# The last rounds of a gather kept free of other stages, and weights loaded within them

## The chip, the cores and the metric

The kernel runs on one core of one Trainium2 chip. The metric is the device time of one execution in microseconds. The core has five engines that run side by side and wait for each other through semaphores: PE (matmuls), DVE and ACT (elementwise work), POOL (which issues the indirect DMAs here) and SP (which issues all other DMAs). Each works through its own stream of instructions in order.

## What is computed

The input x has shape (4, 256, 64, 64): four images of 256 channels and 4096 pixels, in float32. Four layers are applied, each as x = x + layer(groupnorm(x)):

```python
x = x + _L0_conv_ref(_gn(x), ...)   # 1x1 conv, deformable 3x3 sampling, projection, gated feed-forward
x = x + _L1_conv_ref(_gn(x), ...)   # linear attention with a depthwise 5x5 convolution
x = x + _L2_conv_ref(_gn(x), ...)   # 3x3 convolution with binarised weights
x = x + _L3_conv_ref(_gn(x), ...)   # attention over a 2x2 max-pooled image
```

What matters of layer 0 is its second half. A bilinear sampling reads 9 points in each of 4 groups for every pixel, at offsets that the network has computed; the result is projected to 256 channels and added. Then come the gate and the feed-forward:

```python
x2 = _bn(inp + dout, bn2_g, bn2_b, bn2_m, bn2_v, 3)
s = x2.mean((1, 2))
s = jax.nn.relu(s @ se_down_w.T + se_down_b)
s = jax.nn.sigmoid(s @ se_up_w.T + se_up_b)
x3 = x2 * s[:, None, None, :]
hmid = jax.nn.leaky_relu(jnp.einsum('nhwc,oc->nhwo', x3, fc1_w) + fc1_b, SLOPE)
m = jnp.einsum('nhwc,oc->nhwo', hmid, fc2_w) + fc2_b
```

The mean runs over all pixels of an image, so the feed-forward of an image can begin only when its sampling has ended.

## The kernel before

The program is written as Python generators, one for each stage of each image, and a function that takes turns between them. `sample(n)` is the sampling of image n in 288 rounds: 16 blocks of 18 rounds. In a round, POOL issues four indirect DMAs (L607, tile `g`, a ring of seven buffers, so that POOL can be at most seven rounds ahead of PE), and PE turns the four gathered tiles into weighted sums with eight matmuls (L614, into the PSUM banks `acc` and `dp` in turn, two rounds to a bank). After two rounds ACT copies the bank (L619, `at`), PE transposes it (L624), ACT spreads it into `dT` (L634), and at the end of a block PE projects it (L647, `po`), DVE adds it to the image (L653, L654) and ACT finishes it (L658), which also leaves its sum for the mean (`ssum`), and SP writes it out (L661, `x2`). The weights `wm` of the rounds are made by ACT (L599), some rounds ahead; for the first rounds of a sampling all 32 activations stand at its start.

`beside(steps, number, *works)` walks over the rounds of a sampling, and after each round lets the other stages emit their instructions. Each work is a tuple of a generator, its total cost, and the share of the rounds at which it begins and ends. A work emits as long as it has spent less of its cost than its share says; once the share has reached its end, all that is left of it is emitted at once. Inside `ordered()` the order of emission is the order of the instructions on PE, DVE, ACT and POOL. SP's order is left to the scheduler.

The samplings run one after another. Sampling 0 has the first convolutions of the other images beside it. Beside sampling 1 run `binarise`, the feed-forward and the linear attention of image 0. Beside samplings 2 and 3 run the feed-forward and the linear attention of the image before (`behind`), and the 3x3 convolution and the pooled attention of the image before that (`second`). The feed-forward has the rounds up to the share 0.22 (`BEGUN`, round 63), `linear` and `second` the rest up to the end. After sampling 3, a last `beside` over 900 steps without a sampling takes the feed-forward and the linear attention of the last image and what is left of the others.

The emission of `feedforward` begins with two pools of buffers on the right side of SBUF, which take the place of those that `linear` has left, and with four loads: `f1` and `f2` (8 KB in each of 128 partitions, 1 MB each; both stand as `f` in the profile), `sd` and `su`. Then DVE reduces the mean (L712), PE takes it through `sd` (L716) and `su` (L723), ACT makes the gate (L718, L724) and scales `f1` by it (L727), and the blocks follow: L752 and L762 on PE. In the linear attention the last steps on PE are `den` (L938), `rden` (L951) and the projection (L960); in the pooled attention they are L1315, L1327, L1333 and L1343. The weights of the 3x3 convolution, `w2`, are loaded by one DMA of 3 MB (L1051).

Of the kernel before, what the change touches and what calls it, by code (L numbers as in the profile page):

```python
# [18 lines left out]
N, C, H, W = 4, 256, 64, 64  # L19
# [20 lines left out]
CONVOLVE, OFFSETS, BINARY = NB * 9 + 26, 60, 92  # L40
FEED = NB * 40 + 8
LINEAR, LAST = 956, 582
STEPS, BEGUN = 900, 0.22
CONV2, POOLED = 191, 376.5
CONV, SECOND = 150, 568
EPS_BN = 1e-5
# [26 lines left out]
class Net:  # L73
# [625 lines left out]
    def feedforward(self, n, ssum, st):  # L699
        nc, tc, a = self.nc, self.tc, self.a  # L700
        with tc.tile_pool(name=f"fa{n}", bufs=1, side="right") as sp, \
                tc.tile_pool(name=f"fb{n}", bufs=2, side="right") as bp:
            f1 = sp.tile([P, KT, 4 * C], F32, name="f1")
            nc.sync.dma_start(f1, a["fc1_wT"])
            f2 = sp.tile([P, 4 * KT, C], F32, name="f2")
            nc.sync.dma_start(f2, a["fc2_wT"])
            sd = sp.tile([P, KT, 64], F32, name="sd")
            nc.sync.dma_start(sd, a["se_down_wT"])
            su = sp.tile([64, C], F32, name="su")
            nc.sync.dma_start(su, a["se_up_wT"])  # L710
            mean = sp.tile([P, KT], F32, name="mean")
            nc.vector.tensor_reduce(mean, ssum, AX.X, ALU.add)  # L712
            nc.vector.tensor_scalar(mean, mean, 1.0 / HW, None, ALU.mult)
            ps = self.ps()
            for k in range(KT):
                nc.tensor.matmul(ps[0:64, 0:1], sd[:, k], mean[:, k:k + 1], start=k == 0, stop=k == KT - 1)  # L716
            dn = sp.tile([64, 1], F32, name="dn")
            nc.scalar.activation(dn, ps[0:64, 0:1], AF.Relu, bias=self.vec("se_down_b")[0:64])  # L718
            yield 2
            ex = sp.tile([P, KT], F32, name="ex")  # L720
            for m in range(KT):
                ps = self.ps()
                nc.tensor.matmul(ps[:, 0:1], su[:, m * P:(m + 1) * P], dn, start=True, stop=True)  # L723
                nc.scalar.activation(ex[:, m:m + 1], ps[:, 0:1], AF.Sigmoid, bias=self.vec("se_up_b", m))  # L724

            for k in range(KT):
                nc.scalar.activation(f1[:, k], f1[:, k], AF.Identity, scale=ex[:, k:k + 1])  # L727
            yield 6

            waits = []  # L730

            def leave():
                if waits:
                    waits.pop()()

            def hidden(hm, m, ps, t):
                nc.vector.scalar_tensor_tensor(hm[:, m], ps, self.vec("fc1_b", m), t, ALU.add, ALU.max)  # L737

            def total(b, m, ps, xy):
                nc.vector.tensor_tensor(xy[:, m], xy[:, m], ps, ALU.add)  # L740
                if m == KT - 1:
                    self.stats(st, xy, b)
                    nc.sync.dma_start(self.x3_d[n][:, :, b * 512:(b + 1) * 512], xy)

            for b in range(NB):
                x2 = self.block(bp, self.x2_d[n], b, "x2f")
                xy = self.block(bp, self.xy_d[n], b, "xyf")
                hm = bp.tile([P, 4 * KT, 512], F32, name="hm", bufs=1)
                for m in range(4 * KT):
                    ps = self.ps()  # L750
                    for k in range(KT):
                        nc.tensor.matmul(ps, f1[:, k, m * P:(m + 1) * P], x2[:, k], start=k == 0, stop=k == KT - 1)  # L752
                    t = bp.tile([P, 512], F32, name="lk")
                    nc.scalar.activation(t, ps, AF.Identity, bias=self.low1[:, m:m + 1], scale=SLOPE)  # L754
                    leave()
                    waits.append(partial(hidden, hm, m, ps, t))
                    yield 2.5
                leave()
                for m in range(KT):
                    ps = self.ps()  # L760
                    for k in range(4 * KT):
                        nc.tensor.matmul(ps, f2[:, k, m * P:(m + 1) * P], hm[:, k], start=k == 0, stop=k == 4 * KT - 1)  # L762
                        if k % 4 == 3:
                            leave()
                            yield 5
                    waits.append(partial(total, b, m, ps, xy))
            leave()
# [580 lines left out]
    def run(self):  # L1348
        self.setup()
        tile = lambda name, shape: self.cp.tile(shape, F32, name=name)  # L1350
        ssum = [tile(f"ssum{n}", [P, KT, NBLK]) for n in range(N)]
        st = {i: [tile(f"st{i}{n}", [P, KT, NB, 6]) for n in range(2)] for i in (1, 2, 3)}

        feed = lambda n: self.feedforward(n, ssum[n], st[1][n % 2])
        linear = lambda n: self.layer1(n, st[1][n % 2], st[2][n % 2])

        conv = lambda n, side="left": self.layer2(n, st[2][n % 2], st[3][n % 2], side)
        pooled = lambda n, wide=False: self.layer3(n, st[3][n % 2], wide)

        def second(n):  # L1360
            yield from conv(n)
            yield from pooled(n)

        def beside(steps, number, *works):


            spent, open_ = [0] * len(works), set(range(len(works)))

            def advance(share):
                for j in sorted(open_):  # L1370
                    work, total, lo, hi = works[j]
                    while j in open_ and lo <= share and spent[j] < total * (share - lo) / (hi - lo) or share >= hi:
                        cost = next(work, None)
                        if cost is None:
                            open_.discard(j)
                        if not cost:
                            break
                        spent[j] += cost

            for i, _ in enumerate(steps, 1):  # L1380
                advance(i / number)
            while any(works[j][3] <= 1 for j in open_):
                advance(1)

        rounds = NBLK * BR
        E = mybir.EngineType
        ordered = lambda: self.tc.manual_schedule(engines={E.PE, E.DVE, E.Activation, E.Pool})
        behind = lambda n: [(feed(n), FEED, 0, BEGUN), (linear(n), LINEAR, BEGUN, 1)]
        with self.tc.tile_pool(name="gather", bufs=2, side="left") as self.gp, \
                self.tc.tile_pool(name="samp", bufs=2, side="left") as self.sp:  # L1390
            with self.tc.tile_pool(name="pw", bufs=1, side="right") as wp, \
                    self.tc.tile_pool(name="pa", bufs=1, side="right") as sp, \
                    self.tc.tile_pool(name="pb", bufs=2, side="right") as bp:
                w = self.weights(wp)

                pads, used = [], []  # L1400
                convolved = (y for i in range(1, N) for y in self.convolve(i, w, sp, bp, pads, used))
                shifted = lambda first, last: (self.shifts(first, last, w["mw"], bp, pads, used), (last - first) * OFFSETS)
                beside(range(64), 64, (self.convolve(0, w, sp, bp, pads, used), CONVOLVE, 0, 1), (*shifted(0, 1), 0.3, 1))
                with ordered():
                    beside(self.sample(0, ssum[0]), rounds, (convolved, (N - 1) * CONVOLVE, 0, 0.96), (*shifted(1, N * NCH), 0, 1))
            with ordered():
                beside(self.sample(1, ssum[1]), rounds, (self.binarise(), BINARY, 0, 0.2), *behind(0))
                for n in range(2, N):
                    beside(self.sample(n, ssum[n]), rounds, *behind(n - 1), (second(n - 2), SECOND, BEGUN, 1))
        self.idle, self.alone, self.spare = cycle(["acc", "dp"]), True, True  # L1410
        rest = pooled(N - 2)
        with ordered():
            beside(range(STEPS), STEPS, (feed(N - 1), FEED, 0, 0.27), (linear(N - 1), LAST, 0.27, 1), (conv(N - 2), CONV2, 0.27, 0.53), (rest, POOLED, 0.53, 1.02))
        self.spare = False
        self.idle = cycle(["acc", "dp", "vk"])
        fours = self.layer2_fours(N - 1, st[2][1], st[3][1])
        beside(range(STEPS), STEPS, (fours, CONV, 0, 1), (rest, 60, 0, 1))

        self.banks = cycle(["mm", "mm", "mm", "vk"])
        for _ in pooled(N - 1, True):  # L1420
            pass
# [94 lines left out]
```

## Time and profile before

| what | us |
|---|---|
| median of 3 runs | 7441.21 (7437.45 to 7445.19) |
| the profiled execution | 7427.54 |
| its span | 7425.7 |
| PE busy | 5885.9 (79%) |
| DVE busy | 4870.1 (66%) |
| ACT busy | 3564.6 (48%) |
| POOL busy | 4928.8 (66%) |

The span is what the instructions cover; the execution has 1.8 us around it. The four samplings can be told from POOL's gathers: the first begins at 138.5 us, the others at 1598.0, 3051.6 and 4504.2, and the last gather ends at 5976.5. The mean of a feed-forward (L712) is taken at 1617.1, 3073.8, 4548.7 and 6019.9. These four places are called seams in what follows. A row of the timeline gives the start, the length, the engine, the line, the operation with output and inputs, how many such instructions were merged, and in brackets how long the engine sat idle before it and what ended this. A row of the waits gives who waited for what, the sum in us, the number of waits and the longest. A row of busy times by stretch gives the stretch, its length, the busy time of PE, PEld, DVE, ACT and POOL, the share of PE's clock that was granted, the share of the DMA engines' time and GB/s.

### The profile page before, as it was taken

How to read it: one execution, taken by the hardware profiler on the slowest of the kernel's cores; microseconds unless marked ns; L12 is line 12 of the kernel's file. 1: busy time of each engine (PE TensorE's matmuls, PEld its weight loads, DVE VectorE, ACT ScalarE, POOL GpSimd, SP SyncE). 2: the span in 40 equal slices, each digit the busy share in tenths (PEclk: the TensorE clock that was granted, in tenths of full speed). 3: DMA queues.
4: the chain of work that ended last, by engine and by line, in shares of the span. 5: the costliest groups of instructions: out<-in, count | busy, mean ns of one | idle time of the engine just before them, and what ended most of it. 6: DMA issues, size and time to landing. Idle time of an engine off the chain costs nothing. (4 is left out here: it accounts for less than half of the span.)

```text
span 7425.7 us, 98944 instructions
## 1 busy us (share of the span) xinstructions
PE 5885.9 (79%) x35584; PEld 3436.3 (46%) x35584; DVE 4870.1 (66%) x6099; ACT 3564.6 (48%) x10807; POOL 4928.8 (66%) x4850
## 2 busy tenths in 40 slices
PE   5676766569777777898877788988777889977889
PEld 2333333334433333345655444456554444844477
DVE  6455552644488777326989883269998833999863
ACT  2444444445554444455556554554565532655425
POOL 1777777777777777777777776777777710865410
PEclk7776776779877767898988889989889899988899
DMA  6564654666544445555554445555544431210141
GB/s 187 148 191 144 176 173 137 174 183 190 178 127 125 125 125 147 168 156 167 159 155 139 141 147 187 153 167 159 156 142 145 146 115 65 81 54 34 49 124 49
DMA packets 743149, 1037.48 MB, mean 140 GB/s; under 512 B 352000, under 2 KB 457856, under 8 KB 741248
## 3 DMA queue, kind: packets, MB, share of 16 engines
q0 software_dynamic: 221184, 604.27, 27.8%
q1 hardware_dynamic: 521472, 426.87, 19.0%
q8 instruction: 280, 4.59, 0.3%
q14 instruction: 213, 1.74, 0.1%
HBM read 857.44 MB, written 173.33 MB: 139 GB/s over the span
## 5 line engine op out<-in xcount | busy, mean ns | idle before, releaser
L607 POOL DMA_INDIRECT g<-tab,sl x4608 | 4403.3, 956 | 1571.9 <-issue 1285.6
L179 DVE SCALAR_TENSOR_TENSOR agg<-pad,vec,agg 128x1024 f32<-128x1024 f32 x2280 | 2934.3, 1287 | 64.3
L599 ACT ACTIVATE wm<-sl,con 128x48 f32<-128x48 f32 x6144 | 1496.1, 363 | 24.9 <-DMA sl<-sd 11.8
L614 PE MATMUL dp<-g,wm 128*32 128x128 f32 x9216 | 664.2, 317 | 312.2 <-DMA g<-tab,sl 308.7
L614 PE MATMUL acc<-g,wm 128*32 128x128 f32 x9216 | 664.2, 318 | 298.5 <-DMA g<-tab,sl 285.5
L614 PEld LDWEIGHTS dp<-g,wm 128*32 128x32 f32 x9216 | 324.4, 119 | 664.4 <-DMA g<-tab,sl 493.4
L614 PEld LDWEIGHTS acc<-g,wm 128*32 128x32 f32 x9216 | 325.3, 120 | 661.4 <-DMA g<-tab,sl 452.5
L1102 PE MATMUL ps<-xd,w 128*128 128x256 f32 x2304 | 547.1, 386 | 47.9 <-ACT kt L891 38.6
L1102 PEld LDWEIGHTS ps<-xd,w 128*128 128x128 f32 x2304 | 430.5, 193 | 131.7 <-ACT kt L891 40.3
L752 PE MATMUL ps<-x2f,f 128*128 128x512 f32 x1024 | 479.0, 613 | 4.7 <-ACT f L727 4.0
L762 PE MATMUL ps<-hm,f 128*128 128x512 f32 x1024 | 467.7, 604 | 0.0
L837 PE MATMUL ps<-xr,qw 128*128 128x512 f32 x768 | 442.8, 706 | 31.2 <-DMA xr<-x 20.9
L737 DVE SCALAR_TENSOR_TENSOR hm<-ps,vec,lk 128x512 f32<-128x512 f32 x256 | 191.5, 751 | 372.8 <-ACT lk L754 369.2
L619 ACT COPY at<-dp 128x256 f32<-128x256 f32 x288 | 107.3, 373 | 679.9 <-PE dp L614 668.6
L619 ACT COPY at<-acc 128x256 f32<-128x256 f32 x288 | 107.2, 372 | 594.0 <-PE acc L614 584.0
L754 ACT ACTIVATE lk<-ps,low 128x512 f32<-128x512 f32 x256 | 175.7, 688 | 363.1 <-PE ps L752 359.2
L1333 PE MATMUL ps<-gt,pT 128*128 128x129 f32 x2048 | 303.3, 307 | 34.4 <-ACT pT L1329 32.2
L1333 PEld LDWEIGHTS ps<-gt,pT 128*128 128x128 f32 x2048 | 286.7, 219 | 87.5 <-ACT pT L1329 48.7
L647 PE MATMUL po<-dT,ow 128*128 128x288 f32 x1024 | 299.3, 440 | 25.5 <-ACT dT L642 11.6
L1315 PE MATMUL s<-ph,th 128*128 128x512 f32 x512 | 280.7, 659 | 44.9 <-DVE ot L955 13.8
L201 POOL TENSOR_TENSOR ak<-ak,m 128x1024 f32<-128x1024 f32 x96 | 229.0, 2385 | 119.3 <-ACT m L197 115.7
L201 POOL TENSOR_TENSOR av<-av,m 128x1024 f32<-128x1024 f32 x96 | 227.8, 2373 | 113.2 <-ACT m L197 109.2
(286 smaller groups left out, 8337.6 us busy)
## 6 DMA issues: line engine op xcount, KB each, us to landing
g<-tab,sl POOLq DMA_INDIRECT x4608
x<-x SPq DMA_DIRECT2D x112, 512.0 KB
xr<-x SPq DMA_DIRECT2D x96, 512.0 KB
tab<-xo SPq DMA_DIRECT2D x192, 128.0 KB
x<-in_x SPq DMA_DIRECT2D x32, 512.0 KB
y<-yc SPq DMA_DIRECT2D x32, 512.0 KB
yb<-y SPq DMA_DIRECT2D x64, 256.0 KB
x<-yb SPq DMA_DIRECT2D x64, 256.0 KB
```

The lines of the kernel that those rows point to most:

```text
L179: nc.vector.scalar_tensor_tensor(to, s, wt, acc, ALU.mult, ALU.add)
L201: nc.gpsimd.tensor_tensor(acc, acc, made[t - 1], ALU.add)
L599: nc.scalar.activation(wm[:, :, :, o], blocks[b][:, r:r + WR, G:], AF.Copy, scale=self.con("own")[:, o:o + 1])
L607: nc.gpsimd.indirect_dma_start(out=g[:, i, :], out_offset=None, in_=table, in_offset=bass.IndirectOffsetOnAxis(ap=sl.bitcast(I32)[:, r, i: ...
L614: nc.tensor.matmul(acc[32 * i:32 * i + 32, :], wm[:, r4, 4 * i + 2 * x:4 * i + 2 * x + 2, :], g[:, i, x * P:(x + 1) * P], start=x == 0, st ...
L647: nc.tensor.matmul(po[m][:, 0:BR * OB], self.ow[:, k, m * P:(m + 1) * P], dT[b][:, k].rearrange("p r o -> p (r o)"), start=k == 0, stop=k ...
L752: nc.tensor.matmul(ps, f1[:, k, m * P:(m + 1) * P], x2[:, k], start=k == 0, stop=k == KT - 1)
L762: nc.tensor.matmul(ps, f2[:, k, m * P:(m + 1) * P], hm[:, k], start=k == 0, stop=k == 4 * KT - 1)
L837: nc.tensor.matmul(ps, qw[:, k, m * P:(m + 1) * P], x[:, k], start=k == 0, stop=k == KT - 1)
L1102: nc.tensor.matmul(ps[:, e], w[:, k, t, 2 * half + e, m * P:(m + 1) * P], v[:, 2 * half + e, k, t:t + 8], start=i % 6 == 0, stop=i % 6 == 5)
L1315: nc.tensor.matmul(s[i], tv[:, 4 * b + j], ph[:, i * 512:(i + 1) * 512], start=True, stop=True)
L1333: nc.tensor.matmul(ps[:, 0:P + 1], pT[:, m], gt[:, m], start=m == 0, stop=m == 7)
```

## The change

A third mark, `END` = 0.98, takes the place of 1 as the end of `linear` and of `second` beside the samplings. 0.98 of 288 rounds is 282.2, so what is left of them is emitted after the 283rd round. The feed-forwards are made once, in a list, instead of by a function, and `feedforward` has one more stop, after its four loads. `behind` has a third work: the feed-forward of the next image, with the cost 1, from `END` on; its end of 2 is never reached, so only its first step is emitted, the pools and the four loads. The next `beside` takes up the same generator after them.

```diff
-STEPS, BEGUN = 900, 0.22
+STEPS, BEGUN, END = 900, 0.22, 0.98
...
             su = sp.tile([64, C], F32, name="su")
             nc.sync.dma_start(su, a["se_up_wT"])
+            yield 1
             mean = sp.tile([P, KT], F32, name="mean")
...
-        feed = lambda n: self.feedforward(n, ssum[n], st[1][n % 2])
+        feeds = [self.feedforward(n, ssum[n], st[1][n % 2]) for n in range(N)]
...
-        behind = lambda n: [(feed(n), FEED, 0, BEGUN), (linear(n), LINEAR, BEGUN, 1)]
+        behind = lambda n: [(feeds[n], FEED, 0, BEGUN), (linear(n), LINEAR, BEGUN, END), (feeds[n + 1], 1, END, 2)]
...
-                    beside(self.sample(n, ssum[n]), rounds, *behind(n - 1), (second(n - 2), SECOND, BEGUN, 1))
+                    beside(self.sample(n, ssum[n]), rounds, *behind(n - 1), (second(n - 2), SECOND, BEGUN, END))
...
-            beside(range(STEPS), STEPS, (feed(N - 1), FEED, 0, 0.27), (linear(N - 1), LAST, 0.27, 1), (conv(N - 2), CONV2, 0.27, 0.53), (rest, POOLED, 0.53, 1.02))
+            beside(range(STEPS), STEPS, (feeds[N - 1], FEED, 0, 0.27), (linear(N - 1), LAST, 0.27, 1), (conv(N - 2), CONV2, 0.27, 0.53), (rest, POOLED, 0.53, 1.02))
```

The new line in `feedforward` moves all lines behind it by one: L716 of before is L717 of the changed kernel, L1343 is L1344.

## The prediction

> **What bounds the kernel now.** I read the groups by line first, then the waits of PE and of POOL sampling by sampling, then the timelines of PE and POOL at the seams between samplings. The page's costliest groups:
>
> ```profile
> L607 POOL DMA_INDIRECT g<-tab,sl x4608 | 4403.3, 956 | 1571.9 <-issue 1285.6
> L179 DVE SCALAR_TENSOR_TENSOR agg<-pad,vec,agg 128x1024 f32<-128x1024 f32 x2280 | 2934.3, 1287 | 64.3
> ```
>
> POOL issues one gather every 0.95 + 0.30 = 1.25 us, so a round (four gathers) costs it 5.0 us and a sampling (288 rounds) 1441 us; four samplings fill 138 to 5976 us almost without a hole. It looks as if POOL were the bound. PE's waits, by sampling, say otherwise. Sampling 1 from round 63 on (window 1920 to 3050):
>
> ```profile
> PE dp L614 <- DMA g<-tab,sl: 109.5, 156, 1.9
> PE acc L614 <- DMA g<-tab,sl: 98.3, 130, 3.6
> ```
>
> There PE starves for gathered data 286 times: POOL leads. In the same stretch of samplings 2 and 3 (3380 to 4540, 4870 to 6012) no such wait stands among the longest; what stands there is the other stages' work, here of sampling 3:
>
> ```profile
> PE pt L1327 <- ACT pe L1321: 29.0, 15, 4.2
> PE dp L624 <- ACT at L619: 25.3, 11, 9.7
> PE acc L624 <- ACT at L619: 23.7, 12, 8.7
> PE ps L1102 <- ACT kt L891: 19.7, 3, 18.2
> ```
>
> and the busy time of the two stretches (time, PE, PEld, DVE, ACT, POOL):
>
> ```profile
> 3374.00:4542.00 1168.00, 944.04 (x6834) 613.00 (x6832) 985.68 (x1166) 632.80 (x2022) 879.15 (x922) 0.89 0.52 152
> 4856.00:6013.00 1157.00, 934.20 (x6809) 611.23 (x6809) 983.09 (x1160) 630.64 (x2014) 847.44 (x888) 0.89 0.51 151
> ```
>
> PE 81% and DVE 84%, coupled by waits on each other: from round 64 of sampling 2 on the two run behind POOL, and POOL is held by its ring of seven `g` buffers. At the end of sampling 3 POOL is done well before PE:
>
> ```profile
> 5975.51 0.95 POOL L607 DMA_INDIRECT g<-tab,sl  x1 [0.30 <-issue]
> ...
> 6005.57 0.65 PE L614 MATMUL dp<-g,wm 128*32 128x128 f32 x16
> 6006.15 3.70 PE L960 MATMUL ps<-ot,pw 128*128 128x512 f32 x8
> 6010.98 1.98 PE L1343 MATMUL ps<-m,ww 128*128 128x512 f32 x4 [1.13 <-ACT m L1338]
> 6012.80 0.38 PE L624 MATMUL dp<-ident,at 128*128 128x128 f32 x2
> 6014.46 4.15 PE L647 MATMUL po<-dT,ow 128*128 128x288 f32 x16 [1.28 <-ACT dT L642]
> 6027.79 0.56 PE L716 MATMUL ps<-mean,sd 128*64 128x1 f32 x4 [9.18 <-DMA su<-in_se_up_wT]
> ```
>
> PE takes the last round 30 us after its gather (6006.2 against 5976.5), ends the other stages (L1343) at 6013.0, then projects the last block, and waits 9.2 us for the feed-forward's weights. At the seam 2 to 3 the same order costs POOL its only long stops:
>
> ```profile
> 4553.78 0.94 POOL L607 DMA_INDIRECT g<-tab,sl  x1 [13.57 <-PE acc L614]
> ...
> 4564.49 0.94 POOL L607 DMA_INDIRECT g<-tab,sl  x1 [6.01 <-DMA xyf<-x]
> ```
>
> **What the Trainium skill says.** "Perfetto Trace Analysis", Optimization Strategy: where the most contended engine changes over time, take the gaps within the regime concerned. The trace agrees: POOL's 20 us of stops lie at a seam, inside a stretch that PE and DVE set. "TensorE: Matmul & The Clock Gate", The mechanism: matmuls start and end in program order. Hence the gathers' matmuls cannot pass the other stages' in PE's stream; the 30 us lag above is that. "DMA: Bandwidth & Descriptors", Issuing engines are not separate DMA queues: all transfers share the same DMA engines. The trace shows 15.36 MB in 60 us (256 GB/s) at the seam 2 to 3, where the 3 MB of `w2`, the two 1 MB weights and the gathers meet.
>
> **The change, part by part.**
>
> *Weights earlier.* One more yield and one more entry: f1, f2, sd, su are issued when `linear` has ended, ahead of the last five rounds, instead of after them. No transfer is added. On SP they move past `out` and the last `x2` write, nothing that a waiting engine needs at once; the `sl` loads of the next sampling stand before them in both orders. At the last seam `w2` also falls behind the first `x2f` and `xyf`. Removed: PE's 9.18 us wait at the last seam, and the one for `su` at 4561.2 (7.74 us) at the seam 2 to 3. At 0 to 1 nothing moves, as no such entry precedes it (feed-forward 0 has one more unit of cost in 328). What is late next at 2 to 3 is ACT's 32 `wm` activations of the new sampling (7.33 us in one row), behind which L718 is queued.
>
> *Last rounds bare.* In the new order the final `den` (L938 before) comes after round 275, not 280, and `linear` and `second` end between the gathers of rounds 282 and 283 (counted from 0): five rounds of gathers then stand alone, and the same work lies in 219 rounds where it lay in 225. Let X be the end of the other stages' last matmul (6012.96 at the last seam, 4541.80 at 2 to 3).
>
> *X moves little.* PE was never short of data in these stretches, so packing the rounds tighter does not slow or speed the other work; it only takes 5.7 rounds' sampling work out of PE's stream. Per round that is 160.3/225 = 0.71 us of L614 (busy in the window 3374 to 4542), about 0.19 of L624 and 49/225 = 0.22 of waits on `at`: 1.1 us, or 6.3 us for 5.7 rounds if PE alone were the path, 0 if DVE were. Both are near 80%; I take 3 us (own estimate, ends 0 and 6.3). POOL now meets the ring sooner: it loses some 20 us inside samplings 2 and 3 (in sampling 2 before: 11.7 us in 22 waits for L614, of which 0.3 each is the ordinary gap, so 5), in exchange for the 20 us at the seam.
>
> *Last seam.* After X: five rounds at 0.64 us (3.2), three pairs of transposes with their wait on `at` (3 x (0.38 + 0.52), 0.52 as at the end of sampling 0: 2.7), 1.28 for `dT`, 4.15 of L647, 1.25 to the mean, 0.4 to PE: 13.0 us. Before it was 6027.79 - 6012.96 = 14.8. So the removed 9.2 us buy 1.8: the bare rounds take the rest.
>
> *Seam 2 to 3.* PE could start the feed-forward about 6 us earlier, but then POOL leads. PE frees the buffer of round 283 just after X, so POOL can start round 2 of sampling 3 only at X + 0.7, and round 63 ends 62 x 5.0 = 310 us later, plus 2.5 to PE: X + 313. Before, PE came to round 63 (counted by L614's groups in the timeline, 7 us behind POOL) at about 4855, X + 313. So this seam gives only what X itself moved.
>
> *Seam 1 to 2.* Sampling 1 is POOL's own; POOL did not stop at 3051 us, and PE, counted in the same way, is down to 3 us behind POOL by round 55 of sampling 2. Value 0.
>
> Sum: 3 (X of sampling 2) + 3 (X of sampling 3) + 1.8 = 7.8, about 8 us. What follows the last seam (feed-forward, 16.65 us of L752 at once) starts earlier by that and is not changed. The profiled execution is 7427.5 us (span 7425.7 and 1.8 around it), which would become 7419.5; the median of the runs shown is 7441.2, 13.7 above it, so 7433. With both ends of the 3 us: 1.8 to 14.4, so 7427 to 7439 on the median.
>
> **The rivals.**
>
> *POOL is the bound after all.* Then every stop is gain: 23 us at the seam 2 to 3 (1.6 + 13.6 + 6.0 + 0.9 + 1.2), and at the end L716 follows the last gather by 2.5 + 13 + 7 for the catching up, 23 us instead of 6027.8 - 5976.5 = 51. Together 51 us: 7390. For it: the back-to-back gathers. Against it: PE has no wait on `g` in the late stretches. Cases between (the lag shrinks partly) lie between 7390 and 7427.
>
> *The stage work gets longer when packed.* The place is PE's stream in rounds 64 to 282 of samplings 2 and 3. The gathers' matmuls fill pauses of PE there (240 us idle of 1470 in the window 4540 to 6010); with 5.7 rounds fewer among them more of the pauses stand open. If each removed round exposes 1.6 us, X comes 9 us later, twice, less the 1.8: +16, 7457. It decides from about 8.5 us on: X of the changed kernel, counted from round 63, longer than 1176 us.
>
> *The transfers were hidden anyway.* The bare rounds eat exactly what the wait gave, X stays: 0 to -2 us, 7440. For it: DVE at 84 to 90% in these stretches.
>
> **How the numbers follow.** Chances: my forecast 0.52, of which a fifth lies beyond 0.2%; POOL as the bound, wholly or partly, 0.30; longer when packed 0.12; hidden anyway 0.06. 0.2% (15 us, about what a measurement of this kernel can tell from no change) puts the border at 7426. Faster: 0.30 + 0.10 = 0.40; same 0.42 + 0.06 = 0.48; slower 0.12. The range goes from a little below the full POOL case (7386) to 7452, short of the slower one; the forecast's own range is 7427 to 7439.
>
> **What would show it.** Right: five groups of L614 after the last L1344 with no wait on `su`; L717 about 13 us after X; POOL's stops moved from the seam (4553 us) into samplings 2 and 3, some 20 us each, ended by PE; X - round 63 shorter by 0 to 6 us than 1168 and 1157. Wrong: PE waits on `g` in the late part of sampling 3 (then POOL leads and the gain is larger), or X later than before (then packing costs), or a new wait of PE at L717 or L753 for a weight that the 3 MB of `w2` delayed.

## The result: slower, with the stage work of both late samplings 36 us longer

The changed kernel takes 7510.9 us (median of 5 runs, 7508.64 to 7514.51) against 7439.8 (7435.12 to 7445.19, 5 runs) of the kernel before: a ratio of 1.0096, 95% interval 1.0081 to 1.0111. Its profiled execution took 7512.88 us, span 7511.0. The instructions are the same, and so is the work of each engine. These are the two groups of the page that were shown of before, now of the changed kernel (busy, mean ns | idle before):

```profile
L607 POOL DMA_INDIRECT g<-tab,sl x4608 | 4404.6, 956 | 1688.2 <-issue 1277.3
L179 DVE SCALAR_TENSOR_TENSOR agg<-pad,vec,agg 128x1024 f32<-128x1024 f32 x2280 | 2934.6, 1287 | 64.4
```

Busy time has grown by 1.3 and 0.3 us; POOL's idle time by 116. To see where the 85.3 us between the spans (7511.0 - 7425.7) come from, I divided both executions at the same instructions. "Feed" is the first matmul of a feed-forward (L716 before, L717 after), "group norm" the first L121 of the stage work behind it, X the end of the last L1343 (L1344 after), as in the prediction.

| stretch | before | after | difference |
|---|---|---|---|
| start to the feed in sampling 2 | 3079.7 | 3068.7 | -11.0 |
| feed to group norm | 299.9 | 310.7 | +10.8 |
| group norm to X of sampling 2 | 1162.2 | 1198.1 | +35.9 |
| X to the feed (seam 2 to 3) | 19.4 | 21.4 | +2.0 |
| feed to group norm | 294.5 | 301.6 | +7.1 |
| group norm to X of sampling 3 | 1157.3 | 1194.9 | +37.6 |
| X to the feed (last seam) | 14.8 | 12.8 | -2.0 |
| feed to the end | 1397.9 | 1402.8 | +4.9 |

So 73.5 of the 85.3 us lie in the two long stretches between group norm and X, the stage work beside samplings 2 and 3. The busy times by stretch divide each in two: the 3x3 convolution's part, and the pooled attention's part from its first L1315 (L1316 after) on, with the linear attention beside both. The columns are the stretch, its length, busy PE, PEld, DVE, ACT and POOL, PE's granted clock, the DMA share and GB/s. First before, sampling 2:

```profile
3379.60:3897.70 518.10, 423.79 (x3152) 304.70 (x3152) 444.81 (x550) 271.15 (x885) 389.74 (x406) 0.89 0.56 163
3897.70:4541.80 644.10, 516.44 (x3662) 306.89 (x3658) 538.29 (x611) 359.79 (x1132) 485.27 (x512) 0.88 0.49 143
```

Then after:

```profile
3379.40:3899.20 519.80, 421.85 (x3123) 302.99 (x3124) 446.54 (x551) 267.44 (x870) 384.48 (x401) 0.89 0.56 162
3899.20:4577.50 678.30, 520.25 (x3607) 306.77 (x3609) 537.46 (x610) 361.93 (x1140) 468.00 (x495) 0.87 0.45 132
```

The convolution's part is 1.7 us longer. The pooled part has 34.2 us more, with PE busy for 3.8 us more and DVE for 0.8 us less: the new time is waiting. (The granted clock is 0.87 in place of 0.88, but PE's busy time, 3.8 us more, leaves it no large share.) In sampling 3 the pooled part has 31.0 us more, 673.6 for 642.6, and the convolution's part 6.7. Who waits is in the waits of the pooled part of sampling 2 (sum, number, longest). DVE and PE before:

```profile
DVE mx L1316 <- PE s L1315: 30.5, 30, 3.8
DVE rden L1336 <- PE ps L1333: 15.8, 7, 4.7
...
DVE both L641 <- ACT dT L634: 3.1, 2, 1.7
...
PE pt L1327 <- ACT pe L1321: 26.0, 15, 3.6
...
PE ps L1333 <- ACT pT L1329: 8.6, 14, 1.3
```

DVE and PE after:

```profile
DVE rden L1337 <- PE ps L1334: 35.8, 12, 8.1
DVE mx L1317 <- PE s L1316: 28.8, 27, 5.1
DVE both L641 <- ACT dT L634: 14.4, 4, 5.7
...
PE pt L1328 <- ACT pe L1322: 40.4, 19, 9.4
PE ps L1334 <- ACT pT L1330: 22.4, 18, 5.8
```

These are the links of one chain: scores on PE (`s`), their maximum on DVE (`mx`), the exponential on ACT (`pe`), its transpose on PE (`pt`), the copy on ACT (`pT`), the product on PE (`ps`), the reciprocal on DVE (`rden`). Each link crosses to another engine, and each engine has other stages' work in its stream. Two places in the timeline of the changed kernel show what a link can meet. A row is the start, the length, the engine, the instruction, and in brackets the idle time before it. In the first, PE works without a hole and DVE stands for 8.1 us:

```profile
4288.08 0.68 DVE L969 TENSOR_TENSOR xq<-xq,pr 128x512 f32<-128x512 f32 x1
...
4290.25 0.58 ACT L1330 COPY pT<-pt 128x512 f32<-128x512 f32 x1 [0.16 <-PE pt L1328]
...
4291.15 3.90 PE L961 MATMUL ps<-ot,pw 128*128 128x512 f32 x8
...
4294.89 1.95 PE L1334 MATMUL ps<-gt,pT 128*128 128x129 f32 x16
...
4296.88 0.17 DVE L1337 RECIPROCAL rden<-ps 128x1 f32<-128x1 f32 x1 [8.11 <-PE ps L1334]
```

`pT` was ready at 4290.83, but the linear attention's projection (L961, 3.90 us) stands ahead of L1334 in PE's stream. In the second it is the other way round, PE stands for 9.4 us:

```profile
4083.27 3.90 DVE L179 SCALAR_TENSOR_TENSOR agg<-pad,vec,agg 128x1024 f32<-128x1024 f32 x3
...
4087.20 3.94 DVE L179 SCALAR_TENSOR_TENSOR agg<-pad,vec,agg 128x1024 f32<-128x1024 f32 x3
...
4091.05 1.28 DVE L1317 TENSOR_REDUCE mx<-s 128x1 f32<-128x512 f32 x2
...
4092.61 1.26 ACT L1322 ACTIVATE pe<-s,mx 128x512 f32<-128x512 f32 x2 [4.16 <-DVE mx L1318]
...
4093.35 1.12 PE L1328 MATMUL pt<-ident,pe 128*128 128x128 f32 x4 [9.42 <-ACT pe L1322]
```

The maximum stands behind two triples of L179 in DVE's stream. In both places the engine that stood goes on with other work, without a further wait, as soon as the link is through (L179 on DVE at 4296.96, L624 on PE at 4094.26). Each stood for what was at the head of its stream; whether the work behind it had long been ready is not shown.

POOL's waits, after, in the same stretch of sampling 2 (3379 to 4578):

```profile
POOL g L607 <- issue: 243.4, 799, 0.3
POOL g L607 <- PE acc L614: 42.7, 16, 9.8
POOL g L607 <- PE dp L614: 42.2, 22, 8.5
```

And before, those for L614, from 3379 to 4542:

```profile
POOL g L607 <- PE dp L614: 7.0, 10, 3.4
POOL g L607 <- PE acc L614: 5.1, 9, 1.6
```

For L614 that is 84.9 us in 38 waits after; without the ordinary 0.3 us before each gather, 73.5. Before it was 12.1 us in 19 waits, 6.4 above the ordinary. In the changed kernel POOL is held by its ring through this stretch, so it is not the bound there.

The last seam, on PE, after:

```profile
6093.43 1.99 PE L1344 MATMUL ps<-m,ww 128*128 128x512 f32 x4 [0.33 <-ACT m L1339]
6095.35 0.64 PE L614 MATMUL dp<-g,wm 128*32 128x128 f32 x16
...
6102.25 4.15 PE L647 MATMUL po<-dT,ow 128*128 128x288 f32 x16 [1.28 <-ACT dT L642]
6108.18 0.36 PE L717 MATMUL ps<-mean,sd 128*64 128x1 f32 x4 [1.78 <-DVE mean L714]
```

The wait for `su` is gone: L717 follows the mean.

### The profile page after: what moved, and what is told of

Same layout as the page of the kernel before. It is cut to its first block, busy times and chain, and to the rows that moved or that the text cites. A ratio compares the mean times of both kernels' runs of the same rounds, so it can differ in the third digit from the quotient of the medians.

```text
span 7511.0 us, 98925 instructions
## 1 busy us (share of the span) xinstructions
PE 5885.5 (78%) x35584; PEld 3429.8 (46%) x35584; DVE 4873.2 (65%) x6099; ACT 3565.8 (47%) x10807; POOL 4930.5 (66%) x4850
## 4 chain that ended last, share of the span: by engine, by line
PE 29%; DVE 22%; POOL 10%; issue 8%; DMA 5%; ACT 5%; SPq 0%; POOLq 0%; DVEq 0%; ACTq 0%
DVE agg L179 15%; POOL g L607 10%; PE ps L753 4%; PE ps L763 4%; DMA g<-tab,sl 4%; PE ps L961 2%; PE ps L838 2%; PE ps L1334 2%; PE s L1316 2%; PE ps L1212 2%; ACT wm L599 2%; PE po L647 1%; PE dp L614 1%; PE acc L614 1%; DVE mx L1317 1%
## 5 line engine op out<-in xcount | busy, mean ns | idle before, releaser
L179 DVE SCALAR_TENSOR_TENSOR agg<-pad,vec,agg 128x1024 f32<-128x1024 f32 x2280 | 2934.6, 1287 | 64.4
L614 PE MATMUL dp<-g,wm 128*32 128x128 f32 x9216 | 650.9, 317 | 293.6 <-DMA g<-tab,sl 291.7
L614 PE MATMUL acc<-g,wm 128*32 128x128 f32 x9216 | 643.2, 313 | 299.0 <-DMA g<-tab,sl 286.5
L614 PEld LDWEIGHTS dp<-g,wm 128*32 128x32 f32 x9216 | 319.7, 120 | 649.8 <-DMA g<-tab,sl 470.3
L614 PEld LDWEIGHTS acc<-g,wm 128*32 128x32 f32 x9216 | 317.3, 119 | 642.9 <-DMA g<-tab,sl 442.9
L838 PE MATMUL ps<-xr,qw 128*128 128x512 f32 x768 | 459.9, 730 | 55.7 <-DMA xr<-x 21.5
L1334 PE MATMUL ps<-gt,pT 128*128 128x129 f32 x2048 | 306.2, 309 | 62.9 <-ACT pT L1330 60.9
L647 PE MATMUL po<-dT,ow 128*128 128x288 f32 x1024 | 320.5, 464 | 34.0 <-DVE x L1087 15.6
L1334 PEld LDWEIGHTS ps<-gt,pT 128*128 128x128 f32 x2048 | 288.0, 220 | 120.6 <-ACT pT L1330 82.4
L1316 PE MATMUL s<-ph,th 128*128 128x512 f32 x512 | 284.6, 663 | 44.8 <-DVE rd L943 11.1
```

The costliest lines, as they stand in the source:

```text
L179: nc.vector.scalar_tensor_tensor(to, s, wt, acc, ALU.mult, ALU.add)
L614: nc.tensor.matmul(acc[32 * i:32 * i + 32, :], wm[:, r4, 4 * i + 2 * x:4 * i + 2 * x + 2, :], g[:, i, x * P:(x + 1) * P], start=x == 0, st ...
L647: nc.tensor.matmul(po[m][:, 0:BR * OB], self.ow[:, k, m * P:(m + 1) * P], dT[b][:, k].rearrange("p r o -> p (r o)"), start=k == 0, stop=k ...
L838: nc.tensor.matmul(ps, qw[:, k, m * P:(m + 1) * P], x[:, k], start=k == 0, stop=k == KT - 1)
L1316: nc.tensor.matmul(s[i], tv[:, 4 * b + j], ph[:, i * 512:(i + 1) * 512], start=True, stop=True)
L1334: nc.tensor.matmul(ps[:, 0:P + 1], pT[:, m], gt[:, m], start=m == 0, stop=m == 7)
```

## The experiments

Three theories stood at the start. *Packing*: the same stage work in 219 rounds in place of 225 is longer in itself, because it is denser. *Weights*: the early loads hold up other transfers or the engines' queues. *Phase*: neither; the shorter share only shifts the steps of `linear` and `second` against each other and against the rounds, and the pauses of the chain above come out longer or shorter by where they fall. All edits are against the kernel before unless they say "the change with".

Eleven of the eighteen runs landed on chips on which the kernel before itself took 8508 to 8587 us. They are told first and shortly, as they decide nothing about the faster chips.

### Parts of the change on the slower chips

Weights alone, `e1_weights` (again as `e10_weights_again` and `e14_weights_third`): the loads are issued when `linear` has ended after the last round, and the shares stay.

```diff
+            yield 1    (after the four loads; feed-forwards made once, as in the change)
+        behind = lambda n: [(feeds[n], FEED, 0, BEGUN), (linear(n), LINEAR, BEGUN, 1), (feeds[n + 1], 1, 0.9999, 2)]
```

> linear and second end with the last round as before; only the early weights stay, issued after linear's last step and ahead of the sampling's tail. Theory P (the packing of linear and second into 219 rounds lengthens them): the time is that of before or a few us less, 7425 to 7442. Theory W (the early loads hold up SP's queue or the DMA engines): most of the 71 us stays, above 7490.

Packing alone, `e2_packed`, and its two halves, `e3_second` and `e4_linear`:

```diff
+        behind = lambda n: [(feed(n), FEED, 0, BEGUN), (linear(n), LINEAR, BEGUN, 0.98)]        (e2, e4)
+                    beside(self.sample(n, ssum[n]), rounds, *behind(n - 1), (second(n - 2), SECOND, BEGUN, 0.98))   (e2, e3)
```

> Only the end of linear and second at 0.98, weights loaded as before. Theory P: 7505 to 7525, the whole loss and a few us more for the waits on the weights. Theory W: 7435 to 7450.

> Only second ends at 0.98, linear at 1, weights as before. Theory P with the pooled attention's chain as the place (its dependent steps fall closer together): more than half of the loss, 7480 to 7510. If instead linear's DVE work is the place: near before, 7440 to 7455.

> Only linear ends at 0.98, second at 1, weights as before. Theory P with linear's DVE work as the place: 7480 to 7515. With the pooled chain as the place: 7440 to 7460.

| run | us | before, same chip | ratio, 95% interval |
|---|---|---|---|
| e1_weights | 8503.9 | 8508.4 | 0.9997 [0.9989, 1.0005] |
| e2_packed | 8508.6 | 8508.4 | 0.9999 [0.9992, 1.0007] |
| e3_second | 8530.9 | 8508.4 | 1.0024 [1.0016, 1.0031] |
| e4_linear | 8485.5 | 8508.4 | 0.9972 [0.9962, 0.9982] |

No loss of 1% anywhere. But these executions differ from the first already where the edits have changed nothing, from 300 to 900 us, in sampling 0. The kernel before, on the chip of the first measurement:

```profile
300.00:900.00 600.00, 426.18 (x2808) 221.87 (x2809) 294.35 (x424) 252.14 (x927) 455.60 (x475) 0.73 0.58 168
```

e1_weights:

```profile
300.00:900.00 600.00, 299.82 (x2333) 171.55 (x2322) 254.18 (x360) 218.43 (x808) 389.62 (x407) 0.64 0.49 139
```

POOL issued 407 gathers in place of 475, 5.9 us a round in place of 5.05. Its waits over the whole of e1_weights have a line that the waits of the kernel before do not show:

```profile
POOL g L607 <- remote: 690.7, 342, 6.0
```

The expectations of e5 and e11, below, took this for slow gathers that set the pace. The traces do not bear that out. In samplings 2 and 3 PE hardly waits for gathered data (in e1_weights once, 1.1 us, from 3965 to 5333 us), and the other engines have such stops as well:

```profile
ACT at L619 <- remote: 1534.6, 267, 37.4
PE acc L624 <- issue: 180.2, 45, 13.3
```

Over the whole of e1_weights ACT stood 2122.8 us and DVE 718.3 us for "remote", which no engine does in the kernel before, and PE 792 us for "issue", against 6.8. So all engines have stops of many lengths here that the first chip's execution lacks. Why these chips are slower, and why the loss does not show on them, stays open; these four runs say nothing about the loss on the faster ones. (That the two halves have opposite signs, and their sum none, is at least no sign of a price for density.) Seven more runs fell on such chips.

`e7_nudge` is the change with `SECOND` at 571 in place of 568, `e8_before_nudge` the kernel before with it, `e9_end99` and `e13_end99` the change with `END = 0.99`, `e15_begun_nudge` the change with `BEGUN` at 0.2 and `SECOND` at 571; the diffs stand below, where each comes again on a faster chip.

> The whole change with SECOND at 571 instead of 568: density, bare rounds and weights as in the changed kernel, only the rounds in which second's steps fall move a little. Theory P (density): 7505 to 7520. Theory F (phase: which dependent steps of linear and second meet in a round): somewhere else, 7380 to 7550, more than 15 us from 7511.

> The kernel before with SECOND at 571, ends at 1, density and weights as before. Theory P: 7430 to 7450. Theory F: more than 15 us from 7440, on either side.

> The whole change with END at 0.99, half of the packing. Theory P, even in the density: about 7470 (7455 to 7490). Theory F: no such order, any time from 7380 to 7540.

> Weights alone, as e1_weights, on a chip where before takes about 7440. The packed kernel with the weights loaded as before took 7514 beside 7439, the whole change 7511 beside 7440, so theories P and F both: 7430 to 7440, a gain of 2 to 8 us from the wait of 9 us at the last seam. Theory W: 7450 or more.

> As e9_end99 (END at 0.99), for a chip where before takes about 7440. Theory F (phase): no order by density, any time from 7380 to 7520; more than 15 us off 7475, the middle of before and the change, speaks for it. Theory P (density): 7455 to 7490.

> Weights alone, linear and second in the order of before. 7430 to 7440 beside 7440: 2 to 8 us gained. 7450 or more if the early loads cost something themselves.

> BEGUN 0.20, END 0.98 as e6_begun (7378 beside 7439), SECOND at 571. Theory F: more than 15 us from 7378, more likely up, 7395 to 7450, since 7378 is a lucky draw. If the gain of e6 was the structure's (bare rounds at unchanged density): 7365 to 7392.

| run | us | before, same chip | ratio, 95% interval |
|---|---|---|---|
| e7_nudge | 8583.5 | 8582.3 | 1.0001 [0.9991, 1.0011] |
| e8_before_nudge | 8585.6 | 8582.3 | 1.0009 [0.9999, 1.0019] |
| e9_end99 | 8572.0 | 8582.3 | 0.9992 [0.9982, 1.0003] |
| e10_weights_again | 8575.3 | 8582.3 | 0.9993 [0.9983, 1.0003] |
| e13_end99 | 8580.4 | 8587.0 | 0.9994 [0.9987, 1.0001] |
| e14_weights_third | 8584.0 | 8587.0 | 0.9997 [0.9986, 1.0008] |
| e15_begun_nudge | 8556.2 | 8587.0 | 0.9967 [0.9952, 0.9982] |

All lie within 0.35% of before and decide nothing either; the earlier begin alone kept a small gain here.

### Packing alone, and the change with an earlier begin

`e5_packed_again` is e2_packed. `e6_begun` is the change with the stage work begun six rounds earlier, so that it again has 0.78 of the rounds, 224.6, as before:

```diff
-STEPS, BEGUN, END = 900, 0.22, 0.98
+STEPS, BEGUN, END = 900, 0.2, 0.98
```

> The same edit as e2_packed (end at 0.98, weights as before), because in that call the kernel before itself took 8508 us, its gathers stalled in every few rounds, and so said nothing of the case where POOL issues a round every 5.0 us. Where before takes about 7440 us: theory P (packing) 7500 to 7525; theory W (the early loads) 7435 to 7450. Where before takes about 8500 us: the same as before within 10 us by both.

> The whole change, but BEGUN at 0.20, so that linear and second have 0.78 of the rounds as in the kernel before and the feed-forward has 0.20. Theory P, the density itself: the loss is gone, 7425 to 7445 where before takes 7440. If it is not density but how the steps of linear and second fall against the rounds (theory F, phase), any time from 7420 to 7520 is possible, as the start moves by 6 rounds. Theory W: 7500 or more.

Measured, beside 7438.9 of before: e5 7514.4, ratio 1.0103 [1.0074, 1.0133]; e6 7378.2, ratio 0.992 [0.9892, 0.9949]. The packing alone carries the whole loss: its pooled part is 679.5 us in sampling 2, the same as the change's 678.3. The weights theory falls. e5 also shows the seams without the early loads: X to feed takes 26.3 and 14.5 us there, 21.4 and 12.8 in the change. At seam 2 to 3 this is no clean price, since e6, with the early loads, takes 33.9 there. And e6, with the bare rounds and the early loads kept, beats both kernels. It has the density of before, but its stretch from group norm to X is 25 us shorter than before's (1137.3), which equal density does not explain; the packing theory had asked for 7425 to 7445.

### A price moved by half a per cent

If phase is the cause, then an edit that changes neither the share of the rounds nor the work, but shifts `second` a little against the rest, should move the time by as much. `SECOND` is the total cost by which `second` is spread over its rounds. At 571 in place of 568 its steps come up to 0.53% of 219 rounds earlier, 1.2 rounds at the end.

```diff
-CONV, SECOND = 150, 568
+CONV, SECOND = 150, 571
```

`e11_nudge_again` is the change with it, `e12_before_nudge_again` the kernel before with it.

> As e7_nudge (the whole change, SECOND at 571), for a chip where before takes about 7440 us. Theory P (density): 7505 to 7520. Theory F (phase): more than 15 us from 7511, on either side. Where before takes 8500 us and more, nothing is told: gathers set the pace there.

> As e8_before_nudge (the kernel before, SECOND at 571). Theory P: 7430 to 7450. Theory F: more than 15 us from 7440, on either side. Where before takes 8500 us and more, nothing is told.

Measured, beside 7433.2 of before: e11 7453.5, ratio 1.0028 [1.0012, 1.0044]; e12 7488.2, ratio 1.0074 [1.0045, 1.0104]. The same nudge takes 57 us from the change (7510.9, on a chip whose kernel before was 6.6 us slower) and puts 55 us on the kernel before; under it, the packed kernel is the faster of the two by 35 us. The pooled part, e11:

```profile
3894.90:4541.30 646.40, 506.69 (x3590) 302.14 (x3588) 539.96 (x611) 362.10 (x1138) 469.39 (x495) 0.90 0.48 139
```

e12:

```profile
3897.20:4566.90 669.70, 521.99 (x3640) 312.80 (x3636) 540.67 (x611) 360.99 (x1135) 485.20 (x512) 0.87 0.47 138
```

DVE's busy time is 540.0 and 540.7 us, for 538.3 and 537.5 before and after, and the length follows the waits again: DVE's wait of `rden` for `ps` is 15.8 us before, 35.8 after, 19.5 in e11 and 29.2 in e12. The sign of the packing's effect depends on the nudge, so density cannot be its cause in any simple form. (The nudge packs `second` itself, by 1.2 rounds; but it does so in both kernels, and they move in opposite directions.) These are the two runs that decide.

### Half of the packing, the weights alone, and the nudge on the earlier begin

The last three runs fell on a faster chip. `e17_end99_fast` is the change with `END = 0.99`, `e16_weights_fast` is e1_weights, `e18_begun_nudge_fast` is e6_begun with `SECOND` at 571.

> The early weights alone, sampling costs spread to the end as before. If the early weights carry no loss (phase theory and packing theory alike): 7430 to 7440 against 7439, the seams 2 to 3 and the last one shorter by 2 to 4 us each, the stage length from the group norm to the end of the attention as before, 1157 to 1165 us. If early loads disturb the sampling (weights theory): above 7450.

> The change with three bare rounds in place of six (0.99 for 0.98), weights early. Density theory: half of the loss, 7470 to 7480. Phase theory: anywhere from 7400 to 7520, with the pooled part of the stage between 630 and 690 us and VectorE's busy time in it as in all other runs, about 1003 us; a time below 7440 or above 7515 would speak against density outright.

> The change with the stage work begun at 0.20 and the price of the second steps at 571 in place of 568. If the gain of the earlier begin (7378) is that of lower density (less work in each round), it stays under the nudge: 7370 to 7395. If it is phase, the nudge moves it by tens of us: 7410 to 7460, as the nudge moved both other kernels by 55.

Measured, beside 7437.1 of before: e16 7431.4, ratio 0.9996 [0.9987, 1.0005]; e17 7433.8, 0.9997 [0.9988, 1.0005]; e18 7380.2, 0.9928 [0.9911, 0.9945].

e16 moved the loads too little to test them: they are issued after the last round, and PE still waits 8.33 us before L717 at the last seam, for 9.18 before. What clears the loads of the loss is e5.

e17: END at 0.99 leaves two rounds bare in the trace, for five in the change (its expectation counts three and six). Half of the packing has none of the loss, where density asked for half, 7470 to 7480; its 7433.8 us are below the 7440 that the expectation named as the border against density outright. Its two parts in sampling 2:

```profile
3380.80:3887.20 506.40, 417.90 (x3134) 301.93 (x3134) 441.39 (x546) 265.42 (x867) 382.51 (x398) 0.90 0.57 165
3887.20:4543.80 656.60, 523.34 (x3648) 310.02 (x3642) 542.11 (x615) 364.53 (x1145) 482.07 (x510) 0.88 0.47 140
```

The pooled part does lie between before's and the change's, 12.5 us longer, but the convolution's part is 11.7 us shorter; the sum is 1163.0 against 1162.2. DVE is busy for 983.5 us in it, as before (983.1); the 1003 us of the expectation were a slip.

e18: the gain of the earlier begin stays under the nudge (7378.2 and 7380.2). The phase theory had asked for 7410 to 7460, so it missed here, and the expectation put a stable gain down to lower density. But the density is lower only than the change's, not than before's. The traces show another reason: with the earlier begin POOL has become the bound. The gathers of samplings 2 and 3, from the first to the last, take 1450.7 and 1455.8 us in e6 and 1449.3 and 1451.6 in e18, as those of sampling 1, which POOL leads (1453.0 to 1455.3 in these kernels); in the changed kernel they take 1520.9 and 1521.8. POOL's stops for L614 beyond the ordinary 0.3 us come to some 6 us in sampling 3 of e6 and 2 in that of e18, and to nothing in sampling 2. And PE waits for gathered data in the late part of sampling 2, which it does not before. The pooled part of e18:

```profile
PE acc L614 <- DMA g<-tab,sl: 9.3, 12, 1.6
PE dp L614 <- DMA g<-tab,sl: 6.8, 10, 1.8
```

So a nudge of the stage work could slow these kernels, but could hardly speed them up. That it did not slow them is one draw; e18 is weak evidence on phase either way. Its parts in sampling 2:

```profile
3355.90:3845.90 490.00, 413.51 (x3139) 295.40 (x3135) 435.55 (x542) 268.64 (x882) 372.52 (x386) 0.92 0.57 167
3845.90:4491.90 646.00, 514.21 (x3640) 305.79 (x3640) 544.52 (x615) 366.87 (x1160) 488.81 (x517) 0.91 0.49 143
```

The stage work begins at 3355.9, 23.7 us before the kernel before's 3379.6, because there are six fewer feed-forward rounds, 30 us at POOL's pace; PE comes to the group norm 16 us behind POOL's gathers of that round, for 8 before. Then its convolution's part is 28 us shorter. Why that part is shorter I have not shown: its granted clock is 0.92 against 0.89, and DVE has 9 us less work in it, as the border between the parts falls elsewhere.

Sampling 2 of all kernels that ran on faster chips. The fifth column is the sum of four waits of the chain in the pooled part: `mx` for `s`, `rden` for `ps` (DVE), `pt` for `pe`, `ps` for `pT` (PE). Waits of the two engines overlap in part, so the sum is a measure of the pauses, not their length.

| kernel | rounds for the stage work | SECOND | convolution + pooled part | four waits | time |
|---|---|---|---|---|---|
| before | 63 to 288 | 568 | 518.1 + 644.1 | 80.9 | 7439.8 |
| e16, weights | 63 to 288 | 568 | 521.8 + 644.1 | 81.0 | 7431.4 |
| e12 | 63 to 288 | 571 | 516.8 + 669.7 | 106.9 | 7488.2 |
| e17 | 63 to 285 | 568 | 506.4 + 656.6 | 95.7 | 7433.8 |
| after | 63 to 282 | 568 | 519.8 + 678.3 | 127.4 | 7510.9 |
| e5, packed | 63 to 282 | 568 | 519.1 + 679.5 | 131.5 | 7514.4 |
| e11 | 63 to 282 | 571 | 515.1 + 646.4 | 89.9 | 7453.5 |
| e6 | 58 to 282 | 568 | 497.9 + 639.4 | 89.1 | 7378.2 |
| e18 | 58 to 282 | 571 | 490.0 + 646.0 | 77.0 | 7380.2 |

The four kernels with the longest pooled parts have the largest sums, in the same order. DVE is busy for 980 to 984 us of the stretch from group norm to X in all nine.

Shown: the loss comes with the packing, not with the loads; it lies mostly in the pooled part, as waits of DVE and PE on the chain; at the same packing half a per cent of a price removes most of it; and with the earlier begin POOL is the bound. Argued only: that the places shown at 4083 and 4288 us are typical of the added waits. Open: which pair of steps decides, what density by itself costs (e11 is still 20 us above its before, of which the stretch from group norm to X shows none in sampling 2, 1161.5 against 1162.2, and 7.0 in sampling 3; its two seams from X to feed have 11.2 more), why the earlier begin shortens the convolution's part, and why the slower chips do not show the loss.

## Why the prediction was wrong

It said 7433 us, 7386 to 7452; 7510.9 was measured.

*What bounds the kernel* held for the change. POOL's ring held it to PE's pace in both late samplings, more than before, and no wait of PE for `g` is longer than 2.3 us between group norm and X. The rival "POOL is the bound" (0.30) got nothing from this change. But the kernel before stood close to that bound: its gathers of sampling 2 took 1452.3 us, those of sampling 1 1453.3. And e6 and e18, where the stage work begins earlier, reach it: their spans are 50.0 and 57.3 us shorter than before's, where the rival's sum was 51. (The parts differ from its working: L717 follows the last gather by 16.9 and 19.4 us, not 23.)

*X moves little* is the step that failed: "packing the rounds tighter does not slow or speed the other work; it only takes 5.7 rounds' sampling work out of PE's stream", for a gain of 3 us per sampling (0 to 6.3). Measured from group norm to X it was a loss of 35.9 and 37.6 us. The step treated a stretch with PE and DVE both near 80% as a sum of work, of which some goes, and put the cost of re-timing the rest at nothing. But 179 us of the 1162 are DVE's waits (its length less its busy time; 214 after), and the nudges show that they depend on where the steps fall (181 in e11, 205 in e12). That the waits are large was seen (PE's `pt` for `pe`, 29.0 us); that the change re-deals every one of them was not.

The rival *the stage work gets longer when packed* had the right place, rounds 64 to 282 of samplings 2 and 3, and the right sign: X came 1198.1 us after the group norm, beyond its border of 1176. Its price, 9 us a sampling for pauses that stand open for want of gathers' matmuls, was a quarter of what came, and its mechanism is not the one shown: it would not be undone by a nudge that keeps the rounds. With 0.12 it was also held too unlikely.

*POOL would lose some 20 us inside samplings 2 and 3*: 73.5 and 71.8 (82.6 us in 36 waits, less 0.3 each), for the same reason; the direction was right.

*Last seam*: 13.0 us predicted, 12.8 measured (6095.4 to 6108.2), gain 2.0 for 1.8, with the five rounds and the projection in the order that was worked out. e5, without the early loads, has 14.5: nearly what the bare rounds cost, the removed wait gave.

*Seam 2 to 3*: POOL's stop at the seam is gone, and X to feed is 2.0 us longer, as five bare rounds and a projection of 5.84 us take the place of the wait. The next late thing was named: an L614 there waits 4.95 us for `wm`, as before. "X + 313" to round 63 came as X + 323 at the group norm (X + 314 before), a miss of its own: POOL began round 2 at X + 4.8, not X + 0.7, without a stop at the ring just before; its 62 rounds took 312 us, not 310; and the group norm came 6.2 us behind them, not 2.5. *Seam 1 to 2*, value 0: the feed starts 11.0 us earlier and the group norm 0.2. Right.

*The transfers were hidden anyway*: at the last seam nearly so, where the removed wait bought 2.0 us; but this rival had X in its place, and X moved. e16 does not test it, as its loads come after the last round.

## What to carry to other kernels

Where several stages are interleaved in in-order streams and no engine is full, the time of a stretch is busy time plus waits, and an edit to when steps are emitted re-deals the waits: put an uncertainty of the size of the waits' changes on it, not of the work moved. Before such an edit is called good or bad, run it and the baseline with a nudge of half a per cent that moves no work; here the nudge alone was worth 55 us, up or down. Where a gain survives the nudge, see first whether another bound has been reached: the earlier begin kept its gain (0.992 and 0.9928) where the gathers, back to back, set the pace, a floor that both runs reach. How its interleaving would fare above that floor is not shown. And a rival bound that gets nothing from one edit may be the floor for the next.

## What was not expected of the hardware

The same kernel took 7433 to 7440 us on some chips and 8508 to 8587 on others. On the slower ones all engines have stops that the kernel before does not have on the first chip: POOL issued 407 gathers against 475 in the same 600 us, and over e1_weights 690.7 us of POOL's, 718.3 of DVE's and 2122.8 of ACT's stops are put down to "remote". The granted clock was lower too (0.64 against 0.73 in that stretch). The cause is not shown. An edit that lost 1% on the faster chips (e5, 1.0103) lost nothing there (e2, 0.9999), so a null result on one kind of chip says nothing of the other.
